# Batches 2 to 7 of an expert layer: routing tables turned by VectorE and DMA instead of TensorE

## The chip, the cores and the metric

The kernel runs on one core of a Trainium2 chip. The metric is the device time in microseconds of one execution; before the change the median of three runs is 1375.35 us (1374.36 to 1376.78). All data is float32.

## The reference

Eight batches of 256 tokens (width 256) pass through four residual layers: a cross-attention with 16 heads of 16, a soft mixture of experts, a cross-attention with 16 heads of 64, and a gated feed-forward layer. The change touches the second alone:

```python
xn = rmsnorm(x, norm_gamma)                      # x: layer norm of the residual stream
sn = rmsnorm(slot_embeds, slot_norm_gamma)       # 8 experts x 128 slots
logits   = einsum('bnd,esd->bnes', xn, sn)       # 256 tokens x 1024 slots, per batch
dispatch = softmax(logits, axis=1)               # over the tokens
combine  = softmax(logits.reshape(b, n, e*s), axis=-1)   # over the slots
slots = einsum('bnd,bnes->besd', xn, dispatch)
h  = gelu(einsum('besd,edh->besh', slots, w1) + b1)
eo = einsum('besh,ehd->besd', h, w2) + b2
out = einsum('bmd,bnm->bnd', eo.reshape(b, e*s, d), combine)
```

Each batch's logits are needed in two forms: with tokens on the partitions (softmax over slots, table `combine`) and with slots on the partitions (softmax over tokens, table `dispatch`). Both finished tables are then needed in the other form again, because a matmul contracts over partitions.

## The kernel before

The mixture of experts works on groups of two batches (512 tokens), g = 0 to 3. `experts(g)` makes 64 pieces, eight for each of eight experts. A piece is `up(e, hc)`: two matmuls of 128x256 (L964) of the expert's slots with `w1`, and a GELU on ScalarE (L972); and a part of `down`: two matmuls (L980) of an earlier expert with `w2`. The profile counts each such float32 matmul as two instructions. `down` of expert e comes behind `up` of expert e, that is beside `up` of e+1. Its sum is moved out of PSUM by VectorE (L989). `combine` (L1006) makes the layer's output of a group, beside the next group's experts.

`routing(g + 1)` prepares the next two batches while group g's experts run. For each batch:

- `prepare` normalises the tokens and turns them (4 transposes, `pt_xm`).
- `by_token(t)`, for two tiles of 128 tokens: logits `ln` in PSUM, 128 tokens x 1024 slots (L828); maximum (L836), Exp (L839) to `en`, and two copies of the raw logits to `lg` (L846).
- `turn_token(t)`: eight 128x128 transposes of `en` on TensorE against an identity matrix (L854), copied by VectorE (L859) to `CT`, which `combine` reads.
- `by_slot(q)`, for two halves of 512 slots: eight transposes of `lg` (L869) give the logits by slot in PSUM; maximum (L875), Exp on ScalarE (L880), and GpSimd multiplies with the reciprocal of the sums (L888).
- `turn_slot(q)`: eight transposes of that table back (L898), copied to `dt` (L903).
- `fill(q)`: matmuls `pf` of tokens and `dt` (L910), scaled by VectorE into the experts' slots (L918).

Every second piece of `experts` from the tenth on is followed by one piece of routing. Batches 0 and 1 are routed elsewhere (`routing0`, beside the first attention) and stay as they are.

Expert weights live in two sets, `moe_sets[0]` and `[1]`; expert e uses set e % 2. `load_expert` (L217 to L220) issues `w1` (1 MB), `w2` (1 MB) and `b2` on SyncE's DMA queue, called SP below. A load into a set waits until the matmuls that read the set's earlier contents are done. SP handles its instructions in order: a load that waits holds up all that stand behind it.

Every engine handles its own list of instructions in order. The lists are made by a scheduler when the kernel is built: it takes the source's order as priority and may move instructions that are not marked `keep_in_program_order`. DMAs take turns on eight semaphores, and each waits until the DMA that last used its semaphore has landed.

PSUM holds two `big` tiles (128x1024), three `mm` tiles (128x512, two `up` pieces each) and one `o` tile, which `down` uses.

Of the kernel before, what the change touches and what calls it, by code (L numbers as in the profile page):

```python
# [62 lines left out]
def kernel(ctx: ExitStack, tc: tile.TileContext, a: dict, out: bass.AP):  # L63
# [153 lines left out]
    def load_expert(to, e):  # L217
        nc.sync.dma_start(to["w1"], a["w1"][e].rearrange("(c p) f -> p c f", p=P))
        nc.sync.dma_start(to["w2"], a["w2"][e].rearrange("(c p) f -> p c f", p=P))
        nc.sync.dma_start(to["b2"], a["b2"][e].partition_broadcast(P))  # L220

    moe_sets = [moe_tiles(pr, 0)]
    with ExitStack() as l0:
# [546 lines left out]
        at(50, lambda: load_expert(set0, 0))  # L770
# [25 lines left out]
    with ExitStack() as l0f:  # L796
        pm = l0f.enter_context(tc.tile_pool(name="pm", bufs=2))
        moe_sets.append(moe_tiles(l0f.enter_context(tc.tile_pool(name="po", bufs=1)), 1))

        def routing(g):  # L800
# [7 lines left out]
            steps = []  # L808
            for bl in range(2):
# [13 lines left out]
                def by_token(t, b=b, bl=bl, st=st):  # L823

                    pl = ps_big(f"ln_{b}_{t}")
# [11 lines left out]
                    en = pm.tile([P, 1024], F32, tag="em", bufs=4, name=f"en_{b}_{t}")  # L837
# [6 lines left out]
                    for m in range(2):  # L844
                        lg = pm.tile([P, 512], F32, tag="lg", bufs=6, name=f"lg_{b}_{t}_{m}")
                        nc.vector.tensor_copy(lg, pl[:, m * 512 : (m + 1) * 512])  # L846
                        st[f"lg{t}{m}"] = lg

                def turn_token(t, b=b, bl=bl, st=st):
                    for m in range(2):  # L850
                        pt = ps_mm(f"ptn_{b}_{t}_{m}")
                        for i in range(4):
                            e = 4 * m + i
                            nc.tensor.transpose(  # L854
                                pt[:, i * P : (i + 1) * P],
                                st[f"en{t}"][:, e * P : (e + 1) * P],
                                ident,
                            )
                        nc.vector.tensor_copy(  # L859
                            CT[:, bl, 4 * m : 4 * m + 4, t * P : (t + 1) * P],  # L860
                            pt.rearrange("p (e n) -> p e n", e=4),
                        )

                def by_slot(q, b=b, st=st):

                    pl = ps_big(f"ls_{b}_{q}").rearrange("p (i n) -> p i n", i=4)
                    for i in range(4):
                        for t in range(2):
                            nc.tensor.transpose(  # L869
# [57 lines left out]
                for t in range(2):  # L927
                    steps.append([lambda f=by_token, t=t: f(t), lambda f=turn_token, t=t: f(t)])
# [541 lines left out]
```

## Time and profile before

| what | value |
|---|---|
| median of three runs | 1375.35 us (1374.36 to 1376.78) |
| the profiled execution: time, and span from first to last instruction | 1375.81 us, 1373.9 us |
| TensorE busy | 1326.6 us (97%), granted clock 0.987 over the whole span |
| VectorE, ScalarE, GpSimd busy | 575.1, 578.9, 194.6 us |
| the four expert groups (286 to 914 us after the start) | granted clock 1.00 |
| 1 MB weight loads | 64, landing after 6.4 us (median) |

The profile follows one execution. A group of instructions is told by its line, engine, operation and tiles (output, arrow, inputs), with its count and mean duration. "PEld" is TensorE's loading of stationary matrices, which runs beside its matmuls. Matmuls overlap in a pipeline: a group's mean duration is longer than the step from one matmul to the next, so a cost on TensorE is read from the start times in the timeline. A line "A <- B: total, times, longest" of the waits says how long A's engine sat idle until B was done.

### The profile page before, as it was taken

How to read it: one execution, taken by the hardware profiler on the slowest of the kernel's cores; microseconds unless marked ns; L12 is line 12 of the kernel's file. 1: busy time of each engine (PE TensorE's matmuls, PEld its weight loads, DVE VectorE, ACT ScalarE, POOL GpSimd, SP SyncE). 2: the span in 40 equal slices, each digit the busy share in tenths (PEclk: the TensorE clock that was granted, in tenths of full speed). 3: DMA queues.
4: the chain of work that ended last, by engine and by line, in shares of the span. 5: the costliest groups of instructions: out<-in, count | busy, mean ns of one | idle time of the engine just before them, and what ended most of it. 6: DMA issues, size and time to landing. Idle time of an engine off the chain costs nothing.

```text
span 1373.9 us, 19006 instructions
## 1 busy us (share of the span) xinstructions
PE 1326.6 (97%) x7504; PEld 961.3 (70%) x7504; DVE 575.1 (42%) x1172; ACT 578.9 (42%) x1386; POOL 194.6 (14%) x149
## 2 busy tenths in 40 slices
PE   6899999899999999999999999999999999999988
PEld 3556655468678877778767888866667667577767
DVE  5777876523330233321333110025444544554544
ACT  1445444635342254522625222204544534554643
POOL 1000001101010000100001000013332332323514
PEclk9899999999999999999999999999999999999999
DMA  8000000023133323332323325340000000000011
GB/s 250 23 2 1 1 1 1 1 96 131 65 131 131 131 76 119 130 113 83 126 69 130 131 88 173 100 126 1 1 1 1 1 1 1 1 1 1 1 31 54
DMA packets 59112, 86.84 MB, mean 63 GB/s; under 512 B 3344, under 2 KB 49040, under 8 KB 59024
## 3 DMA queue, kind: packets, MB, share of 16 engines
q1 hardware_dynamic: 57440, 84.33, 18.8%
q10 hardware_dynamic: 1584, 1.31, 0.4%
q8 instruction: 59, 0.97, 0.3%
q14 instruction: 29, 0.24, 0.1%
HBM read 83.53 MB, written 2.10 MB: 62 GB/s over the span
## 4 chain that ended last, share of the span: by engine, by line
PE 84%; ACT 6%; DVE 4%; DMA 2%; issue 2%; POOL 1%; SPq 0%; POOLq 0%; ACTq 0%; DVEq 0%
PE ph L964 16%; PE pe L980 15%; PE sc L73 8%; PE q L73 6%; PE o L73 5%; PE po L73 5%; PE k L73 5%; PE pc L1006 4%; PE v L73 4%; PE pe L76 4%; PE ln L828 3%; PE pf L910 3%; ACT ex L1206 2%; PE pf L73 1%; ACT ex L497 1%
## 5 line engine op out<-in xcount | busy, mean ns | idle before, releaser
L972 ACT ACTIVATE ht<-ph,b 128x256 f32<-128x256 f32 x256 | 119.0, 473 | 372.1 <-PE ph L964 371.7
L964 PE MATMUL ph<-slots,w 128*128 128x256 f32 x1024 | 266.8, 384 | 1.1 <-ACT ht L972 0.4
L980 PE MATMUL pe<-w,ht 128*128 128x256 f32 x1024 | 263.3, 381 | 0.0
L964 PEld LDWEIGHTS ph<-slots,w 128*128 128x128 f32 x1024 | 182.4, 189 | 54.4 <-ACT ht L972 21.7
L980 PEld LDWEIGHTS pe<-w,ht 128*128 128x128 f32 x1024 | 192.0, 190 | 29.9 <-DVE slots L989 4.2
L1219 POOL TENSOR_TENSOR ex<-ex,rz 128x1024 f32<-128x1024 f32 x64 | 120.2, 1898 | 224.4 <-DVE rz L1217 219.8
L1206 ACT ACTIVATE ex<-sc,nm 128x256 f32<-128x256 f32 x256 | 117.2, 483 | 45.8 <-DVE nm L1201 44.6
L73 PE MATMUL sc<-KT,QT 17*128 17x256 f32 (+1 forms) x1024 | 105.5, 383 | 5.7 <-DVE NM L486 4.8
L497 ACT ACTIVATE ex<-sc 128x512 f32<-128x512 f32 x128 | 74.6, 596 | 84.4 <-PE sc L73 76.6
L486 DVE TENSOR_REDUCE NM<-sc 128x2 f32<-128x512 f32 x128 | 86.7, 687 | 33.0 <-PE sc L73 28.7
L989 DVE TENSOR_TENSOR slots<-pe,b 128x512 f32<-128x512 f32 x32 | 22.1, 692 | 185.0 <-PE pe L980 185.0
L73 PEld LDWEIGHTS sc<-KT,QT 17*128 17x128 f32 (+1 forms) x1024 | 78.0, 189 | 29.0 <-issue 13.3
L73 PE MATMUL q<-xT,wq 128*128 128x256 f32 x384 | 95.4, 396 | 0.9 <-ACT V L1171 0.9
L73 PEld LDWEIGHTS q<-xT,wq 128*128 128x128 f32 x384 | 71.3, 193 | 27.0 <-issue 13.3
L888 POOL TENSOR_TENSOR es<-es,zs 128x1024 f32<-128x1024 f32 x12 | 22.7, 1893 | 445.8 <-DVE zs L887 445.8
L1201 DVE TENSOR_REDUCE nm<-sc 128x4 f32<-128x1024 f32 x64 | 75.4, 1219 | 6.5 <-PE sc L73 2.8
L73 PE MATMUL po<-wo,ot 128*128 128x256 f32 x320 | 72.6, 382 | 0.0
L76 PE MATMUL pe<-ident,ex 128*128 128x128 f32 x512 | 69.9, 278 | 0.5 <-DVE xT L1121 0.4
L73 PEld LDWEIGHTS po<-wo,ot 128*128 128x128 f32 x320 | 60.1, 190 | 11.3 <-issue 3.6
L1235 ACT COPY et<-pe 128x512 f32<-128x512 f32 x64 | 37.0, 607 | 71.9 <-PE pe L76 71.5
L76 PEld LDWEIGHTS pe<-ident,ex 128*128 128x128 f32 x512 | 56.3, 140 | 14.0 <-issue 8.0
L73 PE MATMUL o<-et,V 128*64 128x256 f32 x512 | 62.8, 385 | 0.9 <-ACT ot L1254 0.9
(186 smaller groups left out, 1642.7 us busy)
## 6 DMA issues: line engine op xcount, KB each, us to landing
w<-in_w_dram SPq DMA_DIRECT2D x64, 1024.0 KB, 6.4
b<-in_b_dram SPq DMA_DIRECT2D x32, 128.0 KB, 6.7
out_dram<-y SPq DMA_DIRECT2D x8, 256.0 KB, 2.1
x_sb<-in_x_dram SPq DMA_DIRECT2D x3, 512.0 KB, 6.1
ctx0T<-in_ctxT_dram SPq DMA_DIRECT2D x4, 256.0 KB, 6.8
ctx1T<-in_ctxT_dram SPq DMA_DIRECT2D x8, 128.0 KB, 5.9
se<-in_slots_dram SPq DMA_DIRECT2D x1, 1024.0 KB, 6.0
wq<-in_wq_dram SPq DMA_DIRECT2D x1, 1024.0 KB, 4.9
```

Source lines behind the costliest of these rows:

```text
L73: tc.keep_in_program_order(nc.tensor.matmul(out, lhsT=lhsT, rhs=rhs, start=start, stop=stop))
L76: tc.keep_in_program_order(nc.tensor.transpose(out, in_, ident))
L486: nc.vector.tensor_reduce(NMs[(2 * b + t // 2) % 2][:, qb, t, HD0 + 1 + 64 * i : 64 * i + 64 : 32], sc[i][:, :, 0, :], AX.X, ALU.max, nega ...
L497: nc.scalar.activation(ex[:, 2 - 2 * i : 4 - 2 * i, :], sc[1 - i][:, :, 1, :], AF.Exp)
L828: nc.tensor.matmul(pl[:, m * 512 : (m + 1) * 512], lhsT=st["xnT"][:, c, t * P : (t + 1) * P], rhs=snT[:, c, m * 512 : (m + 1) * 512], star ...
L964: nc.tensor.matmul(ph, lhsT=c_["w1"][:, c, hc * P : (hc + 1) * P], rhs=slots[e][:, c * 256 : (c + 1) * 256], start=(c == 0), stop=(c == 1),)
L972: nc.scalar.activation(ht, ph, AF.Gelu, bias=b1[:, e, hc : hc + 1])
L980: nc.tensor.matmul(c_["pe"][:, b, :], lhsT=c_["ht"][hc][:, b * SL : (b + 1) * SL], rhs=c_["w2"][:, hc, :], start=(hc == 0), stop=(hc == HI ...
L1006: nc.tensor.matmul(pc[:, :D], lhsT=CT[:, bl, e, t * P : (t + 1) * P], rhs=eos[e][:, bl, :], start=(e == 0), stop=(e == E - 1),)
L1201: nc.vector.tensor_reduce(nm, sc, AX.X, ALU.max, negate=True)
L1206: nc.scalar.activation(ex[:, i, qb, :], sc[:, i, qb, :], AF.Exp, bias=nm[:, i, qb : qb + 1], accum_out=z[:, i, qb : qb + 1],)
L1219: nc.gpsimd.tensor_tensor(ex, ex, rz.rearrange("p h q -> p (h q)").unsqueeze(2).to_broadcast([P, 4, S]), ALU.mult,)
```

## The change

The 48 TensorE transposes of each of batches 2 to 7 go. In their place VectorE turns squares of 32x32 (`nc.vector.transpose`): a 128x1024 table is turned within each square, into a tile `tk` [128, k, t, e, 32]. Square (a, k) of every 128x128 block has then to move from partitions 32a to partitions 32k, and `spread` does that with 16 DMAs on SP (for k and a from 0 to 3), of 32 partitions and 64 KB each, from SBUF to SBUF. Three tables are spread per batch: the raw logits to `ls` (slots on partitions, runs of 1 KB), `en` to `CT` (runs of 128 bytes at the destination), and the slot table back to `dt` (runs of 1 KB). The copies to `lg` and out of the transposes' PSUM tiles go; the logits are turned straight out of PSUM. ScalarE and GpSimd work on `ls` in place.

The routing of a group is written out as a string of pieces, with pauses ("-") between them, in place of a pipeline. Buffers: `em` 4 to 2, `dt` 2 to 1, `ls` 1, `tk` 2; `lg` goes. `load_expert` is split: `load_first` (`w1` of expert e+1) is issued at piece 1 of expert e, `load_second` (`w2`, `b2` of e) at piece 0 of e; before, all three of e were issued at piece 0 of e.

```diff
@@ -214,8 +214,10 @@
             b2=pool.tile([P, D], F32, name=f"b2_{i}"),
         )
 
-    def load_expert(to, e):
+    def load_first(to, e):
         nc.sync.dma_start(to["w1"], a["w1"][e].rearrange("(c p) f -> p c f", p=P))
+
+    def load_second(to, e):
         nc.sync.dma_start(to["w2"], a["w2"][e].rearrange("(c p) f -> p c f", p=P))
         nc.sync.dma_start(to["b2"], a["b2"][e].partition_broadcast(P))
 
@@ -767,7 +769,8 @@
             for step in plan.split():
                 when, _, args = step[1:].partition(".")
                 at(int(when), lambda f=does[step[0]], args=args: f(*map(int, args)))
-        at(50, lambda: load_expert(set0, 0))
+        at(50, lambda: load_first(set0, 0))
+        at(50, lambda: load_second(set0, 0))
 
         turn_back, halves = None, []
         for h in range(8 * B + 12):
@@ -797,6 +800,25 @@
         pm = l0f.enter_context(tc.tile_pool(name="pm", bufs=2))
         moe_sets.append(moe_tiles(l0f.enter_context(tc.tile_pool(name="po", bufs=1)), 1))
 
+
+
+        def squares(name):
+            return pm.tile([P, 4, 2, E, 32], F32, tag="tk", bufs=2, name=f"tk_{name}")
+
+        def turn(tk, t, table):
+            for m in range(2):
+                nc.vector.transpose(
+                    tk[:, :, t, 4 * m : 4 * m + 4, :].rearrange("p k e x -> p e k x"),
+                    table[:, m * 512 : (m + 1) * 512].rearrange("p (e k x) -> p e k x", e=4, k=4),
+                )
+
+        def spread(tk, to, rows="p t e x -> p t (e x)"):
+            for k in range(4):
+                for a in range(4):
+                    nc.sync.dma_start(
+                        to(32 * k, a), tk[32 * a : 32 * a + 32, k, :, :, :].rearrange(rows)
+                    )
+
         def routing(g):
 
 
@@ -805,7 +827,7 @@
             slots = moe_sets[g % 2]["slots"]
             mv, scl = moe_stats[g]
 
-            steps = []
+            does = []
             for bl in range(2):
                 b = 2 * g + bl
                 st = {}
@@ -821,6 +843,7 @@
                     st["xnT"] = xnT
 
                 def by_token(t, b=b, bl=bl, st=st):
+
 
                     pl = ps_big(f"ln_{b}_{t}")
                     for m in range(2):
@@ -834,74 +857,72 @@
                             )
                     nm = stat.tile([P, 4], F32, tag="nm", bufs=4, name=f"nmn_{b}_{t}")
                     nc.vector.tensor_reduce(nm[:, 0:1], pl, AX.X, ALU.max, negate=True)
-                    en = pm.tile([P, 1024], F32, tag="em", bufs=4, name=f"en_{b}_{t}")
+                    en = pm.tile([P, 1024], F32, tag="em", bufs=2, name=f"en_{b}_{t}")
                     z = stat.tile([P, 4], F32, tag="zm", bufs=4, name=f"zn_{b}_{t}")
                     nc.scalar.activation(
                         en, pl, AF.Exp, bias=nm[:, 0:1], accum_out=z[:, 0:1]
                     )
                     nc.vector.reciprocal(rzn[:, 2 * bl + t : 2 * bl + t + 1], z[:, 0:1])
                     st[f"en{t}"] = en
-                    for m in range(2):
-                        lg = pm.tile([P, 512], F32, tag="lg", bufs=6, name=f"lg_{b}_{t}_{m}")
-                        nc.vector.tensor_copy(lg, pl[:, m * 512 : (m + 1) * 512])
-                        st[f"lg{t}{m}"] = lg
-
-                def turn_token(t, b=b, bl=bl, st=st):
-                    for m in range(2):
-                        pt = ps_mm(f"ptn_{b}_{t}_{m}")
-                        for i in range(4):
-                            e = 4 * m + i
-                            nc.tensor.transpose(
-                                pt[:, i * P : (i + 1) * P],
-                                st[f"en{t}"][:, e * P : (e + 1) * P],
-                                ident,
-                            )
-                        nc.vector.tensor_copy(
-                            CT[:, bl, 4 * m : 4 * m + 4, t * P : (t + 1) * P],
-                            pt.rearrange("p (e n) -> p e n", e=4),
-                        )
+                    if t == 0:
+                        st["tk_l"] = squares(f"l_{b}")
+                    turn(st["tk_l"], t, pl)
+                    if t == 1:
+                        ls = pm.tile([P, 8, E, 32], F32, tag="ls", bufs=1, name=f"ls_{b}")
+                        st["ls"] = ls
+                        spread(st["tk_l"], lambda k, a: ls[k : k + 32, a::4, :, :].rearrange("p t e x -> p t (e x)"))
+
+                def turn_token(b=b, bl=bl, st=st):
+
+                    tk = squares(f"n_{b}").rearrange("p k t e x -> p k (t e x)")
+                    tk = tk.rearrange("p k (e t x) -> p k t e x", t=2, x=32)
+                    for t in range(2):
+                        turn(tk, t, st[f"en{t}"])
+                    spread(
+                        tk.rearrange("p k t e x -> p k e t x"),
+                        lambda k, a: CT[k : k + 32, bl, :, :].rearrange(
+                            "p e (t a x) -> p (e t) a x", t=2, a=4
+                        )[:, :, a, :],
+                        "p e t x -> p (e t) x",
+                    )
 
                 def by_slot(q, b=b, st=st):
 
-                    pl = ps_big(f"ls_{b}_{q}").rearrange("p (i n) -> p i n", i=4)
-                    for i in range(4):
-                        for t in range(2):
-                            nc.tensor.transpose(
-                                pl[:, i, t * P : (t + 1) * P],
-                                st[f"lg{t}{q}"][:, i * P : (i + 1) * P],
-                                ident,
-                            )
+                    ls = st["ls"][:, :, 4 * q : 4 * q + 4, :]
                     nm = stat.tile([P, 4], F32, tag="nm", bufs=4, name=f"nms_{b}_{q}")
-                    nc.vector.tensor_reduce(nm, pl, AX.X, ALU.max, negate=True)
-                    es = pm.tile([P, 1024], F32, tag="em", bufs=4, name=f"es_{b}_{q}")
-                    es = es.rearrange("p (i n) -> p i n", i=4)
+                    nc.vector.tensor_reduce(
+                        nm, ls.rearrange("p u e x -> p e u x"), AX.XY, ALU.max, negate=True
+                    )
                     z = stat.tile([P, 4], F32, tag="zm", bufs=4, name=f"zs_{b}_{q}")
                     for i in range(4):
                         nc.scalar.activation(
-                            es[:, i, :],
-                            pl[:, i, :],
+                            ls[:, :, i, :],
+                            ls[:, :, i, :],
                             AF.Exp,
                             bias=nm[:, i : i + 1],
                             accum_out=z[:, i : i + 1],
                         )
                     nc.vector.reciprocal(z, z)
                     nc.gpsimd.tensor_tensor(
-                        es, es, z.unsqueeze(2).to_broadcast([P, 4, S]), ALU.mult
-                    )
-                    st[f"es{q}"] = es
-
-                def turn_slot(q, b=b, st=st):
-                    dt = pm.tile([P, 2, 512], F32, tag="dt", bufs=2, name=f"dt_{b}_{q}")
+                        ls,
+                        ls,
+                        z.unsqueeze(1).unsqueeze(3).to_broadcast([P, 8, 4, 32]),
+                        ALU.mult,
+                    )
+
+                def turn_slot(b=b, st=st):
+                    tk = squares(f"s_{b}")
                     for t in range(2):
-                        pt = ps_mm(f"pts_{b}_{q}_{t}")
-                        for i in range(4):
-                            nc.tensor.transpose(
-                                pt[:, i * P : (i + 1) * P],
-                                st[f"es{q}"][:, i, t * P : (t + 1) * P],
-                                ident,
-                            )
-                        nc.vector.tensor_copy(dt[:, t, :], pt)
-                    st[f"dt{q}"] = dt
+                        nc.vector.transpose(
+                            tk[:, :, t, :, :].rearrange("p k e x -> p k (e x)"),
+                            st["ls"][:, 4 * t : 4 * t + 4, :, :].rearrange(
+                                "p k e x -> p k (e x)"
+                            ),
+                        )
+
+                    dt = pm.tile([P, 2, 4, E, 32], F32, tag="dt", bufs=1, name=f"dt_{b}")
+                    spread(tk, lambda k, a: dt[k : k + 32, :, a, :, :].rearrange("p t e x -> p t (e x)"))
+                    st["dt"] = dt
 
                 def fill(q, b=b, bl=bl, st=st):
                     for c in range(2):
@@ -910,7 +931,9 @@
                             nc.tensor.matmul(
                                 pf,
                                 lhsT=st["xh"][:, t, c * P : (c + 1) * P],
-                                rhs=st[f"dt{q}"][:, t, :],
+                                rhs=st["dt"][:, t, :, 4 * q : 4 * q + 4, :].rearrange(
+                                    "p a e x -> p e a x"
+                                ),
                                 start=(t == 0),
                                 stop=(t == 1),
                             )
@@ -923,23 +946,19 @@
                                 ALU.mult,
                             )
 
-                steps.append([prepare])
-                for t in range(2):
-                    steps.append([lambda f=by_token, t=t: f(t), lambda f=turn_token, t=t: f(t)])
-                for q in range(2):
-                    steps.append(
-                        [
-                            lambda f=by_slot, q=q: f(q),
-                            lambda f=turn_slot, q=q: f(q),
-                            lambda f=fill, q=q: f(q),
-                        ]
-                    )
+                does.append(
+                    dict(P=prepare, T=by_token, A=turn_token, S=by_slot, C=turn_slot, F=fill)
+                )
+
             pieces = []
-            depth = max(len(s) for s in steps)
-            for n in range(len(steps) + depth - 1):
-                for k in range(depth):
-                    if 0 <= n - k < len(steps) and k < len(steps[n - k]):
-                        pieces.append(steps[n - k][k])
+            for step in (
+                "P0 T00 T01 A0 P1 - S00 S01 C0 T10 T11 - F00 F01 A1 - S10 S11 C1 - - F10 F11"
+            ).split():
+                if step == "-":
+                    pieces.append(lambda: None)
+                else:
+                    f, args = does[int(step[1])][step[0]], tuple(map(int, step[2:]))
+                    pieces.append(lambda f=f, args=args: f(*args))
             return pieces, CT, rzn
 
         late = []
@@ -951,10 +970,13 @@
             eos, cur = [], {}
 
             def up(e, hc):
+                w, n = moe_sets[e % 2], g * E + e
+
+                if hc == 0 and n > 0:
+                    load_second(w, e)
+                if hc == 1 and n < 4 * E - 1:
+                    load_first(moe_sets[(e + 1) % 2], (e + 1) % E)
                 if hc == 0:
-                    w = moe_sets[e % 2]
-                    if g or e:
-                        load_expert(w, e)
                     cur[e] = dict(w1=w["w1"], w2=w["w2"], b2=w["b2"], ht=[])
                 c_ = cur[e]
                 if hc % 2 == 0:
```

## The prediction

> **What bounds the kernel now.** I read the totals first, then the four expert groups as stretches of time (columns: length; busy time and instructions of TensorE, its weight loads, VectorE, ScalarE, GpSimd; granted clock; DMA share; GB/s), then the waits, then single rows.
>
> ```profile
> PE 1326.6 (97%) x7504; PEld 961.3 (70%) x7504; DVE 575.1 (42%) x1172; ACT 578.9 (42%) x1386; POOL 194.6 (14%) x149
> ...
> 285.00:450.00 165.00, 164.57 (x732) 126.67 (x732) 44.57 (x93) 68.46 (x131) 7.57 (x4) 1.00 0.37 122
> 450.00:606.00 156.00, 155.73 (x697) 120.66 (x696) 49.68 (x115) 65.51 (x121) 7.57 (x4) 1.00 0.33 108
> 606.00:764.00 158.00, 157.61 (x707) 122.29 (x706) 46.55 (x100) 63.62 (x119) 7.57 (x4) 1.00 0.30 99
> 764.00:914.00 150.00, 150.00 (x684) 126.93 (x682) 13.55 (x30) 34.76 (x69) 0.00 (x0) 1.00 0.43 138
> ```
>
> The first three groups carry the routing that changes. TensorE is busy for 478 of their 479 us at full clock; VectorE for 141, ScalarE for 198. So time is TensorE's work, as long as nothing makes it wait. In this stretch its matmuls waited 0.4 us in all, and SP waited for TensorE, not the reverse:
>
> ```profile
> PE ph L964 <- ACT ht L972: 0.4, 2, 0.3
> ...
> SPq L218 <- PE ph L964: 444.4, 28, 25.6
> SPq L219 <- PE pe L980: 100.5, 30, 23.5
> ```
>
> SP is idle, waiting for a weight buffer, for 545 of 628 us. That idleness is what the change spends.
>
> The price of a transpose comes from the timeline (start, length), its number from the rows of the three tiles:
>
> ```profile
> 341.66 1.04 PE L898 MATMUL pts<-ident,es 128*128 128x128 f32 x8
> 342.53 1.03 PE L964 MATMUL ph<-slots,w 128*128 128x256 f32 x4
> ...
> L854 PE MATMUL ptn<-ident,en x96: 272/273/273, 315.0 to 734.6; 128*128 128x128 f32 x96
> L869 PE MATMUL ls<-ident,lg x96: 272/273/273, 318.9 to 739.2; 128*128 128x128 f32 x96
> L898 PE MATMUL pts<-ident,es x96: 272/273/273, 333.2 to 748.0; 128*128 128x128 f32 x96
> ```
>
> Eight transposes take 342.53 - 341.66 = 0.87 us, 0.109 each; the 273 ns are pipeline length. The same timeline gives 0.43 us for a 128x256 matmul (four `ph` records, two matmuls, in 0.87) and 0.86 for 128x512.
>
> **1. TensorE loses work.** 288 x 0.109 = -31.3 us, all on the path. Some blocks cost 0.94 instead of 0.87 (one at 333.21, the next work at 334.15); if all 36 did, -33.8. I take -31.3.
>
> **2. VectorE breaks even.** A batch loses 12 copies of 128x512 (4 `lg`, 4 `CT`, 4 `dt`) at 0.68 = 8.2 us. It gains turns: 4 of 128x512 out of PSUM at 0.717 (first row below), 4 from SBUF at about 0.70, and 2 of 128x1024 at 1.3 to 1.4, scaled from the two sizes in the trace (256: 436 ns, 512: 717): 2.9 + 2.8 + 2.7 = 8.4. At 30% busy this costs nothing. A turn three times as slow would add 17 us per batch, 100 in all, to an engine with 338 us to spare; its delays, not its load, would then show. The Trainium skill (VectorE: DVE Perf Modes, Rules for kernel authors) says to transpose 128x128 on TensorE if PSUM will do as destination. It speaks against the change; but that rule prices one transpose, and here VectorE has the spare time and TensorE none: by the rows -31.3 us against +1.2 off the path.
>
> ```profile
> L534 DVE STREAM_TRANSPOSE zt<-o x16: 706/717/718, 63.0 to 276.1; 128x512 f32<-128x512 f32 x16
> L903 DVE COPY dt<-pts x24: 659/681/692, 334.0 to 748.5; 128x512 f32<-128x512 f32 x24
> ```
>
> **3. SP gets 288 more DMAs.** This is the disputed cost. Nearest rows: small DMAs back to back on SP.
>
> ```profile
> 20.45 4.78 SPq L279 DMA_DIRECT2D wo<-in_wo_dram  x8
> 14.07 1.11 SPq L232 DMA_DIRECT2D ctx1T<-in_ctxT_dram  x2
> 28.30 2.15 SPq L220 DMA_DIRECT2D b<-in_b_dram  x1
> ...
> w<-in_w_dram SPq DMA_DIRECT2D x64, 1024.0 KB, 6.4
> ```
>
> Eight issues in 4.78 us, two in 1.11: 0.55 to 0.60 us each, the last of them 0.47 apart. I take s = 0.57 per spread DMA. A batch then holds SP for 48 x 0.57 = 27 us, a group for 55; with its weight issues (24 at about 0.4) 65 of some 150 us. It fits on average, so the queue's order decides.
>
> In the built order of the first group SP has: `w1` of expert 3, 16 DMAs to `ls`, 16 to `CT`, and only then `w2` of expert 2. TensorE needs that `w2` 48 matmuls of 0.43, 8 of 0.86 and 4 transposes after the `up` of expert 1, where `w1` of 3 goes out: 20.7 + 6.9 + 0.4 = 28.0 us. The queue needs 3 us (VectorE's maximum and turns of the last logits), 32 s, and 6.4 for the load: 9.4 + 32 s. They meet at s = 0.58, or 0.66 if TensorE is itself held up by the 2.4 us of step 4. Such 32 in a row stand twice per group (`ls` + `CT`; `dt` + the next batch's `ls`). So beyond about 0.66 the loss is 6 places x 32 x (s - 0.66) = 192 (s - 0.66); the whole gain is gone at s = 0.78, and at s = 1.0 the kernel loses 65 - 24 = 41 us. At my s the cost is 0, with hardly any cover left.
>
> What may raise s are the `CT` DMAs: 512 pieces of 128 bytes each, 32 on each of 16 DMA engines. In the trace's DMA packet records a 256-byte packet takes 18 ns and an 8-byte one 9; 128 bytes lie near 14: 32 x 14 = 0.45 us, just under the issue time. The row of 2.15 us shows that SP is held when the queues are full. The Trainium skill (DMA: Bandwidth & Descriptors, Specifications) says that under 512 bytes a DMA reads, modifies and writes: at twice the time, 0.9 us per `CT` DMA (estimate), s averages 0.73 in the three rows of `ls` + `CT` and takes 3 x 32 x 0.07 = 7 us back. No row here shows a transfer from SBUF to SBUF. The same page (Rules for kernel authors) calls transfers under 64 KB mostly overhead, 2.0 us fixed (Anatomy of one DMA): paid one after another, 96 us per batch would make SP the bound and the kernel 100 us slower. The `wo` row refutes the serial reading: eight went out in 4.78 us though each landed after 2.5. I weigh the rows more, and keep s from 0.47 to 1.0 for the range.
>
> **4. ScalarE is held longer at a time.** It has as many Exps and fewer table loads, so its sum doesn't grow. But both halves' by-slot Exps now come in a row, since both wait for the same spread: 8 x 0.45 + a table load 1.28 + one GELU 0.37 + table load 1.28 + the by-token Exp 1.11 + table load 1.28 = 8.9 us with a single GELU in it. TensorE has about 7 us of logits and `up` matmuls in that place before its PSUM tiles run out: 1 to 2.4 us lost. I count 1.2 for each of six batches: +7 us (0 to 15).
>
> **5. At nothing.** The weight loads' new places: no load is late before (SP waits for TensorE), so alone they gain 0; they spare `w1` a place behind a spread. Without them a `w1` could stand behind 32 s = 18 us. The single `ls` and `dt`: their reuse waits for GpSimd (two products of 1.89) and for `fill`, both done before the next batch's turn; if not, the SP queue behind is late and step 3 applies. VectorE's maximum waits for 16 landings of `ls`, and the move of `pe` out of its only PSUM tile stands behind it: the spread lands after 16 s + 2.5 = 12 us, and the next `pe` comes an expert, some 19 us, later.
>
> Sum against the profiled execution: 1375.8 - 31.3 + 7 = 1351.5; the median is 0.5 lower: **1351 us**.
>
> **The rivals.**
> - *Full gain, about 1344 (0.05).* ScalarE's bunches find cover. For: 0.4 us of waiting now. Against: 8.9 us without GELUs.
> - *Late spreads take half, about 1362 (0.12).* s near 0.7, or VectorE waiting for landings with `pe` behind it: 4 to 8 us more in steps 3 and 5.
> - *SP is the bound (0.25), slower: about 1390, to 1420.* Issues or 128-byte pieces cost more than the loads' rows show; `w2` comes late and TensorE stands at L1002. It decides from s = 0.78 (for `CT` alone, from 1.2 with the others at 0.57); s = 0.86 gives 1351 + 38 = 1389. For: 32 in a row before a `w2`, no SBUF-to-SBUF row. Against: 0.47 to 0.60 in every back-to-back row.
> - *No change (0.03).* TensorE's work is certainly less, so this is only the middle of the last two.
>
> **How the numbers follow.** The forecast has 0.55 (1343 to 1358). A measurement of this kernel can tell about 0.2% from no change, 2.75 us. Faster: 0.55 + 0.05 + 0.12 = 0.72; same 0.03; slower 0.25. The range runs from 1343 (full gain) to 1395, which leaves out about half of the slower case and almost nothing below.
>
> **What would show it.** Step 1: matmul rows `ptn`, `ls`, `pts` gone from 285 on, TensorE's busy time there about 31 us less. Step 2: VectorE's busy time as before, turns of 128x512 at 0.7. Step 3: SP's spreads every 0.5 to 0.6 us and no TensorE wait for a DMA; waits at L1002 prove me wrong. Step 4: 5 to 10 us of TensorE waits for ScalarE's GELU (L994). The prediction fails if s exceeds 0.66, most likely at `CT`.

## The result, and the profile after

The changed kernel takes 1375.39 us (median of 20 runs, 1372.13 to 1381.54), the kernel before 1374.85 us (median of 20 runs beside them, 1372.66 to 1377.51). The ratio is 1.0006, with a 95% interval of 0.9996 to 1.0016: no change. The forecast was 1351 us. The profiled execution of the changed kernel took 1375.42 us, with a span of 1373.6 us.

The totals and the shares of the chain of work that ended last, on the page of the changed kernel, and below them the same shares before:

```profile
PE 1302.9 (95%) x7216; PEld 937.8 (68%) x7216; DVE 572.2 (42%) x1160; ACT 564.2 (41%) x1374; POOL 194.8 (14%) x149
PE 70%; SPq 9%; DMA 7%; ACT 6%; DVE 5%; issue 2%; POOL 1%; POOLq 0%; ACTq 0%; DVEq 0%
...
PE 84%; ACT 6%; DVE 4%; DMA 2%; issue 2%; POOL 1%; SPq 0%; POOLq 0%; ACTq 0%; DVEq 0%
```

TensorE has the 288 instructions fewer that the change promised (7504 to 7216). But its share of the chain falls from 84% to 70%, and SP's queue and DMAs, 2% of it before, now hold 16%. The same four stretches as in the prediction (length; busy time and instructions of TensorE, its weight loads, VectorE, ScalarE, GpSimd; granted clock; DMA share; GB/s):

```profile
285.00:450.00 165.00, 153.05 (x619) 115.98 (x619) 41.61 (x83) 62.08 (x126) 7.54 (x4) 0.98 0.54 152
450.00:606.00 156.00, 148.86 (x609) 113.21 (x608) 48.73 (x111) 61.33 (x118) 7.58 (x4) 0.99 0.53 152
606.00:764.00 158.00, 151.82 (x614) 116.31 (x613) 44.10 (x89) 58.78 (x115) 7.58 (x4) 0.97 0.52 147
764.00:914.00 150.00, 150.00 (x681) 126.09 (x679) 15.83 (x40) 34.36 (x68) 0.00 (x0) 1.00 0.40 132
```

In the three stretches with routing TensorE is busy for 453.7 of 479 us, so it is idle for 25.3, against 1.1 before; and its clock is below 1.00. The fourth stretch, which has the same experts but no moves, is as it was. The waits of TensorE and of SP in the expert stage of the changed kernel (total, times, longest):

```profile
PE pe L1002 <- DMA w<-in_w_dram: 13.9, 6, 2.8
PE ph L986 <- ACT ht L994: 5.4, 5, 3.0
PE ph L986 <- DMA w<-in_w_dram: 4.9, 3, 3.4
...
SPq L218 <- PE ph L986: 259.2, 21, 22.4
...
SPq L818 <- DMA w<-in_w_dram: 17.6, 9, 3.2
```

TensorE waits 18.8 us for weight loads and 5.4 us for GELUs. SP waited 545 us for TensorE before and waits 287 us now (259 at L218, 27 at L221). The last line is the one to remember: nine times a move of a table (L818) waited for a weight load to land, which it doesn't read. The DMAs take turns on eight semaphores, so a move cannot go out until the load eight DMAs ahead of it has landed. In the first group, for instance, the `w1` issued at 339.32 landed at 351.36, and the move eight DMAs behind it went out at 351.37.

The rest of the time is clock. Six times in the three stretches the granted clock is 0.50 (third number from the end) for 3.41 us, twice back to back; a row for one such stretch, one for the double one, and the sum over all of them:

```profile
398.81:402.23 3.42, 3.34 (x8) 2.69 (x9) 0.00 (x0) 0.47 (x1) 0.00 (x0) 0.50 0.33 81
740.14:746.97 6.83, 5.84 (x13) 4.25 (x14) 0.00 (x0) 0.00 (x0) 0.00 (x0) 0.50 0.82 245
sum 20.49, PE 19.25 PEld 14.48 DVE 0.54 ACT 7.26 POOL 2.67; mean PE 3.85 PEld 2.90 DVE 0.11 ACT 1.45 POOL 0.53
```

TensorE is busy for 19.25 us of them at half the clock, so they cost 9.6 us. The timeline below agrees: the 18 instructions from 375.10 on take 5.57 us until the next one starts (380.67), against 3.9 at the prediction's 0.43 us for two.

The transposes were worth more than the 31.3 us of the prediction. One of the kernels below (a quarter of the moves done by VectorE, later start) lacks the same 288 transposes and runs these stretches at full clock; TensorE's total on its page is:

```profile
PE 1292.7 (96%) x7216; PEld 932.6 (69%) x7216; DVE 601.9 (45%) x1232; ACT 563.6 (42%) x1374; POOL 194.6 (14%) x149
```

1326.6 - 1292.7 = 33.9 us, 0.118 per transpose. So the sum closes: -33.9 us of transposes, +24.2 us of idle time (25.3 - 1.1) and +9.6 us of half clock make -0.1, and the two spans differ by -0.3 us. That gain and loss cancel is chance.

The Trainium skill (TensorE: Matmul & The Clock Gate, Part 1: The HAM clock gate) states a window of 3413 ns and half the clock after an idle one; the stretches agree with both numbers. But single waits of 2.4 and 2.8 us, shorter than the window, were enough here, and so were two of 1.0 and 1.2 us within 4 us (ahead of 375.2), while waits of 3.0 us (ahead of 341.91) and 2.4 us (ahead of 557.59) were not followed by a slow stretch.

Now SP's own queue in the first group of the changed kernel (start, length, instruction; L818 the moves, L221 `w2`, L218 `w1`):

```profile
314.24 10.34 SPq L818 DMA_DIRECT2D ls<-tk_l  x16
324.68 11.03 SPq L818 DMA_DIRECT2D CT<-tk_n  x16
335.81 0.56 SPq L221 DMA_DIRECT2D w<-in_w_dram  x1
...
340.41 16.66 SPq L818 DMA_DIRECT2D dt<-tk_s  x16
357.18 10.17 SPq L818 DMA_DIRECT2D ls<-tk_l  x16
367.45 0.53 SPq L221 DMA_DIRECT2D w<-in_w_dram  x1
...
369.20 18.14 SPq L818 DMA_DIRECT2D CT<-tk_n  x16
387.44 0.57 SPq L221 DMA_DIRECT2D w<-in_w_dram  x1
...
389.23 15.33 SPq L818 DMA_DIRECT2D dt<-tk_s  x16
```

Sixteen moves to `ls` with nothing in the way take 10.2 to 10.4 us, 0.64 each, and sixteen to `CT` 10.7 to 11.0. Sixteen moves that follow a set of weight loads take 15 to 18 us here, and 12 to 17 in the other two groups. All 18 rows of this kind sum to 230.9 us, 0.80 per move. From the first move to the last of the first group SP is at it for 81.7 of 90.3 us (rows of moves over the time from 314.24 to 404.56), a share of 0.90. SP's waits for landings are part of these rows. And TensorE's waits by place, from its timeline (idle time before the matmuls, in brackets):

```profile
375.10 5.73 PE L1002 MATMUL pe<-w,ht 128*128 128x256 f32 x18 [1.22 <-DMA w<-in_w_dram]
393.57 1.97 PE L1002 MATMUL pe<-w,ht 128*128 128x256 f32 x8 [2.39 <-DMA w<-in_w_dram]
398.89 4.49 PE L986 MATMUL ph<-slots,w 128*128 128x256 f32 x12 [3.35 <-DMA w<-in_w_dram]
```

The first waits for the `w2` that went out at 367.45, behind `dt` and `ls`; the second for the one of 387.44, behind the second batch's `CT`; the third for the `w1` after it. The first `w2`, of 335.81, was in time. The other two groups show the same two places.

### The profile page after: what moved, and what is told of

Read it like the earlier page. It is cut to its first block, busy times and chain, and to the rows that moved or that the text cites. A ratio compares the mean times of both kernels' runs of the same rounds, so it can differ in the third digit from the quotient of the medians.

```text
span 1373.6 us, 18749 instructions
## 1 busy us (share of the span) xinstructions
PE 1302.9 (95%) x7216; PEld 937.8 (68%) x7216; DVE 572.2 (42%) x1160; ACT 564.2 (41%) x1374; POOL 194.8 (14%) x149
## 4 chain that ended last, share of the span: by engine, by line
PE 70%; SPq 9%; DMA 7%; ACT 6%; DVE 5%; issue 2%; POOL 1%; POOLq 0%; ACTq 0%; DVEq 0%
PE ph L986 11%; PE pe L1002 11%; SPq L818 8%; PE sc L73 8%; PE q L73 6%; PE o L73 5%; PE po L73 5%; PE k L73 5%; PE pc L1028 4%; DMA w<-in_w_dram 4%; PE v L73 4%; PE pe L76 4%; PE pf L931 2%; ACT ex L1228 2%; PE ln L851 1%
## 5 line engine op out<-in xcount | busy, mean ns | idle before, releaser
L1002 PE MATMUL pe<-w,ht 128*128 128x256 f32 x1024 | 262.5, 389 | 13.9 <-DMA w<-in_w_dram 13.9
L986 PEld LDWEIGHTS ph<-slots,w 128*128 128x128 f32 x1024 | 187.7, 191 | 67.5 <-ACT ht L994 26.2
L1002 PEld LDWEIGHTS pe<-w,ht 128*128 128x128 f32 x1024 | 197.2, 194 | 48.4 <-issue 10.1
L906 POOL TENSOR_TENSOR ls<-ls,zs 128x1024 f32<-128x1024 f32 x12 | 22.7, 1894 | 430.2 <-DMA CT<-tk_n 364.2
```

What stands on the lines that cost most here:

```text
L986: nc.tensor.matmul(ph, lhsT=c_["w1"][:, c, hc * P : (hc + 1) * P], rhs=slots[e][:, c * 256 : (c + 1) * 256], start=(c == 0), stop=(c == 1),)
L1002: nc.tensor.matmul(c_["pe"][:, b, :], lhsT=c_["ht"][hc][:, b * SL : (b + 1) * SL], rhs=c_["w2"][:, hc, :], start=(hc == 0), stop=(hc == HI ...
```

## The experiments

Theory A: the moves make the weight loads late through SP's queue. Theory B: ScalarE and VectorE come late. Theory C: the moves' packets take the DMA engines' time, whoever issues them. "Load waits" below is the sum of TensorE's waits for `w` in the expert stage of the profiled execution.

**The loads' new places alone.** The kernel before, with `load_first` and `load_second` as in the change.

> The kernel before with the two loads of an expert's weights put where the changed kernel has them (w1 one expert ahead, at its second piece; w2 and b2 at its first), and nothing else. Theory A (SP's queue of moves delays the weight loads) and theory B (ScalarE's bunched Exps) both expect no difference, 1374 to 1376 us: before, no matmul of the expert stage waits for a load. If the new places alone made w2 late, it would be 1380 or more, with TensorE waiting at its down matmul for a DMA.

Measured: 1375.58 us, ratio to before 1.0006 (0.9997 to 1.0014), no load wait. The new places neither gain nor cost by themselves.

**Fewer moves: the token tables back on TensorE.**

```diff
-                    spread(tk.rearrange(...), lambda k, a: CT[k : k + 32, bl, :, :]...)
+                    for t in range(2):
+                        for m in range(2):
+                            pt = ps_mm(f"ptn_{b}_{t}_{m}")
...
+                            nc.vector.tensor_copy(CT[:, bl, 4 * m : 4 * m + 4, t * P : (t + 1) * P], ...)
```

> The changed kernel with the token tables (CT) turned on TensorE again, so 96 of the 288 transposes come back and 96 of the 288 moves are gone from SP. Theory A (SP's queue delays w1 and w2): the transposes cost 96 x 0.109 = 10.5 us, and most of the 25 us of TensorE's idle time and the 7 us of the half clock go: 1355 to 1366 us. Theory B (ScalarE's bunched Exps and VectorE's latency make TensorE wait): nothing of the idle time goes, so 1380 to 1386 us. Theory C (the moves' packets hold up the DMA engines): as A, since these are the moves of 128-byte packets.

Measured: 1355.45 us, ratio 0.9865 (0.985 to 0.988). No load wait is left; TensorE is idle for 4.3 of the 479 us; all twelve spreads take 10.2 to 11.2 us, 0.648 per move. Two thirds of the 33.9 us are 22.6; less 3.2 us of idle time more than before, that is 19.4, and the kernel is 19.2 us faster than the one before (1374.66 beside it). B falls as the main cause: ScalarE has the same Exps here and VectorE about as much work (139.8 us in the three stretches against 134.4). A and C both expected this.

**The same moves from another queue.** `CT`'s 96 moves issued by `nc.gpsimd.dma_start`.

> The changed kernel with the 96 moves of the token tables issued from GpSimd's queue instead of SP's; the bytes, packets and landing places are the same. Theory A (time and order on SP's queue): SP is free 16 x 0.65 us earlier for each of the six batches and the weight loads no longer stand behind these moves, so 1347 to 1360 us. Theory C (the packets hold up the DMA engines, whoever issues them): no difference from the changed kernel, 1372 to 1380 us. Theory B: no difference either; GpSimd's own work might come late and then it is slower than 1380.

Measured: 1383.61 us, ratio 1.0062 (1.0043 to 1.0081): a miss for A. TensorE's waits:

```profile
PE ph L987 <- ACT ht L995: 15.3, 12, 3.1
PE pe L1003 <- DMA w<-in_w_dram: 6.5, 2, 6.0
```

The load waits fall from 18.8 to 6.5 us, but waits for GELUs rise from 5.4 to 15.3. In the built order ScalarE now changes between Exp and GELU, with a function-table load of 1.28 us each way: 56 table loads for L995, L899 and L862 in the three stretches against 40 in the changed kernel. The edit moved two things, so it doesn't decide between A and C.

**Only the moves, no gain.** The kernel before with the new load places, 48 moves per batch of the same shapes that nothing reads, and one GELU buffer fewer.

> The kernel before with the new load places and with 48 moves per batch put in at the same points on SP's queue (16 after the last Exp of the logits, 16 after the token tables, 16 after the slot tables, the same shapes and packets), whose landing place nothing reads; one buffer of GELU's output fewer, for room. All transposes stay on TensorE. Theory A: the moves alone make w2 and w1 late, by about as much as they cost in the changed kernel, 20 to 35 us: 1394 to 1410 us, with TensorE's idle time behind DMA. Theory B: nothing waits for these moves, so 1374 to 1380 us.

Measured: 1392.74 us, ratio 1.013 (1.0113 to 1.0146): 18 us slower, just short of the range. The mechanism is not A's, though:

```profile
PE pts L922 <- POOL es L912: 3.5, 1, 3.5
PE ls L893 <- ACT en L859: 2.7, 1, 2.7
```

There is no load wait; 3.9 us more are waits of 0.8 us for VectorE's move of `pe`, and all idle time in the three stretches is 12.0 us. With 3.4 us at half clock that makes some 14 of the 18 us; the rest is open. The added moves read `en` and `es`, and may have kept those buffers from the next tables; that was not tried apart. In this kernel's order the sixteens stand further apart, with loads between them, and they take 0.78 to 0.85 of SP's time between the first and the last of a group. At 0.82 us per move they are no quicker than in the changed kernel, so slow moves alone do not make a load late; what stands ahead of it, and how soon it is needed, count too.

**Another order.** `A0` two places later in the string, so that the first `w2` goes out ahead of `CT`.

```diff
-                "P0 T00 T01 A0 P1 - S00 S01 C0 T10 T11 - ..."
+                "P0 T00 T01 P1 - A0 S00 S01 C0 T10 T11 - ..."
```

> The changed kernel with one thing else: in the written order the first batch's turn of its token tables (A0) stands two places later in each group (behind P1 and the empty place), so that on SP's queue w2 and b2 of the expert at hand stand ahead of these 16 moves and not behind them. Moves, bytes and instructions are the same. Theory A (w2 late because it is queued behind 32 moves): the first batch's share of the loss goes, 1350 to 1364 us. Theory B (ScalarE) and theory C (the DMA engines' time for the packets): nothing changes, 1371 to 1380 us.

Measured: 1377.71 us, ratio 1.0022 (1.0013 to 1.0031): slower than before, a miss for A as it was put. The queue of this run in the first group:

```profile
316.91 10.34 SPq L818 DMA_DIRECT2D ls<-tk_l  x16
327.35 0.53 SPq L221 DMA_DIRECT2D w<-in_w_dram  x1
...
328.63 12.73 SPq L818 DMA_DIRECT2D CT<-tk_n  x16
...
370.54 18.57 SPq L818 DMA_DIRECT2D CT<-tk_n  x16
```

The first `w2` is out 8.5 us sooner (327.35 against 335.81), but it had not been late. The later places are as before, and so are the load waits, 16.5 us. The profile is of the slowest of the 20 executions (1385.33 us), so its 9.8 us of waits for GELUs need not be typical. The loss does not hang on this one place in the order.

**The token tables by VectorE alone.** A VectorE transpose of 32 partitions may write another quarter than it reads, so `CT` needs no DMA: 32 transposes of 32x256 per batch.

```diff
...
+                        for k in range(4):
+                            for a in range(4):
+                                nc.vector.transpose(
+                                    to[32 * k : 32 * k + 32, a, :, :],
+                                    en[32 * a : 32 * a + 32, k, :, :],
+                                )
```

> The changed kernel with the token tables turned and moved between the quarters by VectorE alone: 32 transposes of 32x256 per batch that read one quarter of the partitions and write another, with no DMA; the two halves of the tables are two pieces of the written order. TensorE keeps none of the 288 transposes and SP has 192 moves left of 288. Theory A: SP as in the kernel with the token tables on TensorE, which had 5 us of idle time, and its 10.5 us of transposes saved as well: 1342 to 1352 us. VectorE gets 192 x about 0.41 us = 79 us for 16 us, which its idle 480 us of the stage hide. Theory B (VectorE's and ScalarE's latency): these bursts of 13 us make evictions late, over 1362 us.

Measured: 1377.66 us, ratio 1.0029 (1.0019 to 1.0039), a miss for A. The load waits are gone, and another wait has their place, at the same matmul; below it VectorE's timeline at the longest of them:

```profile
PE pe L1001 <- DVE slots L1010: 18.3, 8, 4.6
...
531.56 7.14 DVE L883 STREAM_TRANSPOSE CT<-en 32x256 f32<-32x256 f32 x16
538.73 0.69 DVE L1010 TENSOR_TENSOR slots<-pe,b 128x512 f32<-128x512 f32 x1
```

The move of `pe` out of its only PSUM tile stands behind 16 transposes of 0.434 us. VectorE's total (219 us in the four stretches of 629 us) is no trouble; the 7.1 us in one piece are. Waits for GELUs, 9.5 us, come on top.

**The same moves in long packets.** `CT`'s moves land in runs of 2 KB instead of 128 bytes (the tables of batches 2 to 7 then stand in the wrong order).

> The changed kernel with the 96 moves of the token tables landing in one run of 2 KB for each partition instead of 16 runs of 128 bytes (the tables of batches 2 to 7 are then in the wrong order, so the kernel's result is not the reference's); number, place and bytes of the moves are the same. Theory A (issue time and order on SP): no change, 1370 to 1380 us. Theory C (the DMA engines' time for small packets): the engines lose 96 x 512 packets of 12 ns over 16 engines, 0.37 us of each move, and TensorE's waits shrink by half or more: 1352 to 1364 us.

Measured: 1372.32 us, ratio 0.998 (0.9968 to 0.9992): 3 us less than the changed kernel, with 14.5 us of load waits and 0.771 us per move. The packets are at most a small part: the runs of this kernel lie between 1365 and 1376 us. C falls as the main cause.

**`CT` from GpSimd's queue, written behind the slot tables, and all moves from it.** The first is the earlier run with `A0` and `A1` behind `C0` and `C1`; the second has `ls` and `dt` from GpSimd's queue too.

> The token tables' 96 moves on GpSimd's queue again, but their turn (A0, A1) written behind C0 and C1, so that GpSimd's multiplications for the slot tables stand ahead of them and ScalarE's Exps stay in the changed kernel's order (as many function-table loads as it has). Theory A, now as SP being full over the stretch of the routing (6 x 16 moves of 0.64 us or more in some 88 us, with 1 MB loads between): SP has two thirds of the moves left, as in the kernel with the token tables on TensorE, and the waits for loads fall from 18.8 us to under 3; ScalarE's 5 us of waits stay; 1345 to 1356 us. Theory C (the DMA engines): no change from the changed kernel, 1370 to 1380 us. Theory B (ScalarE): above 1365 us.

> As the run beside it, with all 288 moves on GpSimd's queue and only the weight loads on SP's. Theory A: no wait for a load at all, since no load stands behind a move; GpSimd gives 288 x 0.65 us = 187 us to the moves, out of some 600 idle us of the stage; 1345 to 1358 us. Theory C: the same packets run beside the same loads, so the loads land as late as in the changed kernel and it stays at 1368 to 1380 us.

Measured: 1362.66 us, ratio 0.9912 (0.9896 to 0.9929), for the first; 1410.55 us, ratio 1.0255 (1.0235 to 1.0275), for the second. Both are over A's ranges, and in both the load waits all but vanish (1.6 us, and none). TensorE's main waits and its load wait in the first, and its main wait in the second:

```profile
PE pf L932 <- DMA dt<-tk_s: 7.2, 4, 3.5
PE pf L932 <- issue: 4.0, 1, 4.0
...
PE ph L987 <- DMA w<-in_w_dram: 1.6, 1, 1.6
```

```profile
PE pf L932 <- DMA dt<-tk_s: 55.0, 4, 18.7
```

The weight loads' time from issue to landing (last number, median) in the changed kernel and in the first run:

```profile
w<-in_w_dram SPq DMA_DIRECT2D x64, 1024.0 KB, 7.1
w<-in_w_dram SPq DMA_DIRECT2D x64, 1024.0 KB, 7.0
```

The bytes and packets are those of the changed kernel, and in the first run a load takes as long to land, 7.0 us against 7.1; still the weights come in time, so what made them late is when SP issues them. This settles A against C for the main part. (The second run says less: its 55 us of other waits give every load time.) But now `fill` waits for `dt`: in the first run one of its moves landed 7.3 us after its issue (527.30) while GpSimd's `CT` moves ran beside it (520.88 to 532.32, DMA share 0.88 around that time), and with all moves on GpSimd, `dt` stands in one queue with `CT` and `ls` and behind GpSimd's own products. The other queue moved the wait instead of removing it. Putting the weight loads, and not the moves, on another queue was not tried, and neither was another number of semaphores; how much of SP's delay is the semaphores' alone stays open.

**A quarter of the moves taken off SP.** The four of each sixteen that stay in their quarter become VectorE copies.

```diff
...
+                    if a == k:
+                        nc.vector.tensor_copy(to(32 * k, a), part)
+                    else:
+                        nc.sync.dma_start(to(32 * k, a), part)
```

> The changed kernel with the four of each 16 moves that stay in their quarter of the partitions (a = k) done as copies on VectorE: 72 of the 288 moves leave SP, evenly over the three tables, and no transpose comes back. VectorE gets 72 x about 0.4 us = 29 us. Theory A (SP full): SP has 48 to 50 us of moves left in each group's stretch of 88 us instead of 62 and more, between the changed kernel (all) and the kernel with the token tables on TensorE (two thirds): half or more of the 32 us lost comes back, 1347 to 1362 us. Theory B: no change or slower, 1372 to 1382 us.

Measured: 1366.66 us, ratio 0.9947 (0.9932 to 0.9962). The load waits are gone, but the time is 4.7 us over A's range, because ScalarE comes to the front in the first group:

```profile
PE ph L988 <- ACT ht L996: 19.4, 12, 7.2
...
384.84 1.28 ACT L900 ACT_TABLE_LOAD   x1
386.14 0.51 ACT L900 ACTIVATE ls<-ls,nms 128x256 f32<-128x256 f32 x1
...
386.75 1.28 ACT L996 ACT_TABLE_LOAD   x1
```

An Exp, then a GELU, and a table load for each. Of the 21.8 us idle 17.6 lie in the first stretch (165.0 - 147.43), 4.2 in the next two. The first group's routing starts five places sooner than the others', which have five pieces of `combine` first.

**The same, and the first group's routing begun five places later; and the later start alone.**

```diff
-            side = list(ending)
+            side = list(ending) or [lambda: None] * 5
```

> The kernel with a quarter of the moves done by VectorE, and the routing of the first group begun five places later (as in the other groups, where five pieces of combining stand ahead of it). In the run without the later start, 16 of TensorE's 22 idle us lie in the first group, behind ScalarE's queue of Exps, and under 2 us in each of the other two. Theory A' (SP full was the first loss, ScalarE's order in the first group is what is left): the first group becomes like the others, 6 to 8 us of idle time and the half clock gone: 1344 to 1353 us. If the first group's wait has another cause than its place: 1362 to 1370 us as without it.

> The changed kernel with the routing of the first group begun five places later and all 288 moves still on SP's queue. Theory A' : SP stays full, so the waits for loads stay (18 us) and with them most of the loss: 1366 to 1377 us. Theory B (ScalarE's order in the first group is the main loss): as the run beside it, under 1356 us.

Measured: both together 1346.22 us (1344.99 to 1349.9), ratio 0.980 (0.978 to 0.9819); the later start alone 1374.63 us, ratio 1.000 (0.999 to 1.001). Both as expected by A. The waits and the three stretches of the first:

```profile
PE ph L988 <- ACT ht L996: 5.7, 10, 1.0
...
285.00:450.00 165.00, 162.59 (x682) 125.71 (x681) 53.83 (x113) 64.27 (x129) 7.53 (x4) 1.00 0.52 157
450.00:606.00 156.00, 153.79 (x642) 118.71 (x641) 59.12 (x136) 63.61 (x123) 7.57 (x4) 1.00 0.49 145
606.00:764.00 158.00, 156.08 (x654) 120.88 (x653) 56.33 (x121) 60.59 (x119) 7.57 (x4) 1.00 0.48 143
```

No load wait, 6.5 us idle, full clock. This kernel beats both: 28.2 us under before (1374.38 beside it), where the transposes' 33.9 less 5.4 us of added idle time give 28.5. With SP full, the later start gains nothing, since the load waits stay (21.6 us).

How full SP is tells most of these runs apart. The share is the rows of moves over the time from the first to the last move, in the three groups:

| run | share of SP's time | load waits, us | median, us |
|---|---|---|---|
| changed kernel | 0.90, 0.89, 0.89 | 18.8 | 1375.39 |
| later start alone | 0.91, 0.91, 0.89 | 21.6 | 1374.63 |
| other order | 0.81, 0.90, 0.89 | 16.5 | 1377.71 |
| long packets | 0.89, 0.90, 0.87 | 14.5 | 1372.32 |
| moves added to before | 0.78, 0.83, 0.85 | 0 | 1392.74 |
| quarter by VectorE, later start | 0.77, 0.75, 0.75 | 0 | 1346.22 |
| `CT` on TensorE | 0.48, 0.56, 0.57 | 0 | 1355.45 |
| `CT` from GpSimd, first run | 0.46, 0.47, 0.47 | 6.5 | 1383.61 |

The share is in part an effect, since it holds SP's own waits behind loads: at 0.64 us, 96 moves would take 61 of the 84 to 90 us, about 0.7. The last row is the exception: nearly all of its 6.5 us is one wait of 6.0, for a `w2` that went out at 368.22, behind `dt` and the next `ls`, and took 10.6 us to land while GpSimd's `CT` moves ran beside it (362.78 to 373.12). So in that one place the DMA engines' time, C, is likely to have a part. A first group at 0.81 (other order) waited, and groups at 0.83 and 0.85 (moves added to before) did not, so no exact limit follows from this.

## Why the prediction was wrong

The likeliest case failed, at step 3, which put SP's moves at nothing: they cost 28.4 us, 18.8 of TensorE's waits for weight loads and 9.6 of the half clock that followed. The rival "SP is the bound" named the mechanism and the place (L1002), but called it slower, 1390 to 1420. "No change" had 0.03; that the loss came out as large as the gain is chance. It is also chance that the rival's formula, with the measured mean of 0.80, gives 192 x 0.14 = 27 us: it has no term for the clock, and place by place it does not fit (below).

**Step 1 held, and was too small.** The three kinds of transposes are gone, and with them 33.9 us, not 31.3: the upper figure, 33.8, was right.

**Step 2 held.** VectorE is busy for 150.3 us in the four stretches against 154.4 before. Its turns in the changed kernel (busy time in all, mean ns of one, idle time before):

```profile
L810 DVE STREAM_TRANSPOSE tk_l<-ln 128x512 f32<-128x512 f32 x24 | 15.3, 686 | 0.7 <-DMA w<-in_w_dram 0.2 <-DMA dt<-tk_s 0.2 <-issue 0.2
L810 DVE STREAM_TRANSPOSE tk_n<-en 128x512 f32<-128x512 f32 x24 | 15.0, 674 | 0.0
L916 DVE STREAM_TRANSPOSE tk_s<-ls 128x1024 f32<-128x1024 f32 x12 | 14.2, 1224 | 12.1 <-POOL ls L906 12.1
```

0.67 to 0.69 us against the 0.70 to 0.717 taken, and 1.22 against 1.3 to 1.4. That VectorE's delays, not its load, would show was seen as a main wait in one experiment only, the bursts of 7 us.

**Step 3 failed, in three ways.** First, s. The prediction took 0.57 from the `wo` row. With nothing in the way it was 0.64, and over all moves 0.80. A line for the tile `wo` before and one for `CT` after show why (issue: shortest, median, longest in ns; landing in us):

```profile
L279 SPq DMA_DIRECT2D wo<-in_wo_dram x8: 312/364/545, 20.4 to 24.8; - x8
...
L818 SPq DMA_DIRECT2D CT<-tk_n x96: 585/628/3611, 324.7 to 733.6; - x96
...
DMA to landing us min/median/max: 2.1/2.1/10.3
```

The issues of `wo` took 0.36 us in the median; 1.4 us of its 4.78 are three waits for earlier loads to land. So the row was no price of an issue: the semaphores' waits were already in it, and that 0.57 is near 0.64 is luck. For `CT` the median issue is 0.63 us, the longest 3.6. So s is not a constant. Of the 46.6 us over 288 x 0.64, waits for the landing of `w` and `b` make 19.5 and most of the rest is issues that take long behind loads. The prediction's own row of 2.15 us for one issue and the semaphore rule in the kernel's description held both, and neither was put into s.

Second, the places. At the first (`ls` + `CT`) s was 0.65 to 0.67 and no `w2` was late, as the limit of 0.66 has it. At the second (`dt` + `ls`) s was 0.84, 0.70 and 0.70; the formula gives 32 x (0.18 + 0.04 + 0.04) = 8.3 us and the waits were 1.2 + 2.4 + 2.4 = 5.9. The third was not in the list: the second batch's `CT` alone, 16 moves at 1.0 to 1.1 us behind `w2`, `b2` and `w1`, with waits of 2.4, 2.8 and 2.8 at L1002 and 3.4 for a `w1`. The remaining 1.6 us are two small waits for `w1`. Looking only for 32 in a row missed it.

Third, a wait of this kind can have a second price that the sum had no term for: the clock, 9.6 us.

The average taken as a check, 65 of some 150 us per group, was the wrong denominator: the moves do not lie over the whole group but over 84 to 90 us of it.

The fears about packets were rightly set aside. `CT`'s 128-byte pieces cost 3 us in the kernel's time (the run with long packets); with nothing in the way their moves went out every 0.67 us, where the doubled time had been put at 0.9, and a packet of 128 bytes took 11 ns (median of the packet records), not 14. A serial 2.0 us per move is not seen either, on SP or on GpSimd's queue (0.53 to 0.65 per move).

**Step 4 held in size.** 7 us were taken for waits for GELUs, at 1.2 for each of six batches; 5.4 came, 3.0 of it in one wait. It was also right that ScalarE is the next limit: it came to 19.4 us as soon as SP was relieved without a later start.

**Step 5.** The new load places are at nothing, as the run with them alone shows. `ls` and `dt` as single buffers stand behind none of TensorE's waits in the changed kernel.

With the measured terms: 1375.8 - 33.9 (step 1) + 5.4 (step 4) + 18.8 (loads) + 9.6 (clock) = 1375.7, against 1375.4 measured.

## What to carry to other kernels

A queue's room has to be counted over the stretch in which the new DMAs are issued, and with the price of a small DMA behind large ones, not of small ones among themselves; here a share of 0.89 on SP, its waits for landings counted in, was too much and 0.75 was not. When a full queue is relieved, ask which engine is next: taking moves away from SP showed ScalarE, VectorE or `dt` in most runs, and only relieving SP and giving ScalarE a better place together brought nearly the whole gain. Idle gaps of 2 to 3 us on TensorE can cost more than their length, since the clock may drop for the 3.4 us that follow. And a row of back-to-back issues has to be split into issues and waits before it is used as a price.

## What the runs showed of the hardware

- A DMA of 64 KB from SBUF to SBUF, 32 partitions wide, holds SP for 0.60 us, and 16 in a row go out every 0.64 (0.67 with runs of 128 bytes); from GpSimd's queue 16 took 8.4 to 10.4 us. It lands after 2.0 to 2.9 us in the median of the three tables, and after up to 11.2 us behind weight loads.
- VectorE moves 32 partitions to another quarter while it transposes: 0.434 us for 32x256. A copy of 32x512 within a quarter, between two tiles, took 0.41 to 0.42 us.
- With SP full, the times scatter more: 1372.1 to 1381.5 us for the changed kernel and 1372.4 to 1385.3 for the other order (20 executions each), against 1371.5 to 1377.2 for the kernel before (44 executions). The cause was not looked for.
